# Byte stores of a top-k moved three steps later, and the first loads, masks and transpositions of the next stage one step sooner

## The chip, the cores and the metric

The kernel runs on one NeuronCore of a Trainium2 chip. The metric is the device time of one execution in microseconds (us). Engines are named as the profile names them: PE (matrix products and transpositions), DVE, ACT and POOL (elementwise work), SP (it issues nearly all DMA transfers here). PEclk is the TensorE clock that was granted, as a share of full speed.

## What is computed

One transformer layer over 2 x 1024 tokens of width 1024, inner width 2752. First a gated MLP whose gate keeps only the larger half of its values in each row, then a layernorm; then an MLP with low-rank additions, and a second layernorm.

```python
s = silu(einsum('bsh,ih->bsi', x, w_gate))
_, idx = top_k(-abs(s), k)                 # k = 2752 // 2, the smallest |s|
s = s.at[rows, idx].set(0.0)
s = s * einsum('bsh,ih->bsi', x, w_up)
h = layernorm(x + einsum('bsi,hi->bsh', s, w_down))
gate = silu(qlora(h, w1q, a1, b1))
y = qlora(gate * qlora(h, w3q, a3, b3), w2q, a2, b2)
out = layernorm(h + y)                     # qlora: tiled base weight plus 0.5 * h A^T B^T
```

All inputs are float32. The kernel splits each operand into a high and a low part and sums three products (high x high, high x low, low x high), so each product is issued three times.

## The kernel before

The 2048 tokens are 16 tiles of 128, in four groups of four (`GT = 4`). Three stages follow one another on PE.

**gate_up** walks a list of steps (group g, unit u, "g" or "u", k), with four units of 688 columns in a group. A unit has seven gate products (k = 0 to 6), formed with sums and differences of operands so that seven do the work of eight, and four up products (k = 0 to 3). L353 issues a product's matmuls of 344 columns: for each of two outputs eight with the high weight and the two parts of x alternately and, at the end, four with the low weight, as the code of `products` orders them; a step of an up product issues two such sets. Weights are loaded by SP into `wr` and split by ACT (`wh`, L173) and POOL (`wl`, L174). Four sums of weights (T1 to T4) were written to DRAM once and are read straight into `wh` and `wl` (L258). Results go to DRAM by SP (L387): `s_d`, the silu of the gate, and `m_d`, its product with the up part, not yet cut.

**The top-k** of a group is the generator `topk`. It finds for each row a threshold by passes that count (on ACT, DVE), one step of it being handed out per product step (L338 to L340; two at up products with even k), so that group g - 1 is thresholded while group g is multiplied. Its end: DVE writes one byte per value, keep or not (L513), into `kv`; then comes a section that all engines enter together, in which DVE reads a flag and a rare exact fallback may run (L530 to L534); then each of the group's four byte tiles is stored to DRAM, `k_d`, one store to a step (L536 to L539). The store is issued behind the last load that was noted (`lastd`). For the last group the same generator runs inside down: from item 12 of the first group on, one step to an item.

**down** multiplies by `w_down`. Its items are (block of inner width `DB`, tile), 24 to a group. An item loads a piece of `m_d` (L710) and of `k_d` (L711), turns the bytes to bf16 on ACT (L724), multiplies on POOL (L725), transposes on PE (L745), takes the high part `mh` on ACT (L749) and the low part `ml` on DVE (L750), runs the products against pieces of `w_down` (L765, 512 columns) and adds their sum to the accumulator on DVE (L768). The accumulator starts as a tile of x, loaded by SP (L775).

The first three items of down, the **early** ones, are prepared inside gate_up. `down(0, early=3)` is a generator that the last unit of the last group advances (L341 to L346). Its first `next` issues the loads of the three items; they go into slices of a tile `em` in the room of a buffer of the top-k (`a0`). The second issues their masks (L724, L725), the third their transpositions and the writing of `eh` and `el` (L745, L749, L750). Their products follow when down starts. Items 1 and 3 use the same PSUM tile for their transpositions.

After a group's last item comes a layernorm, and the finished tile is stored as `x_d`. When the last group's top-k has been used up, `dots_down` (L639, L815 to L838) begins: it reads `x_d` back and forms the row sums of the low-rank parts on DVE (L837), one or two steps to an item (L644, L645); what is left is run at L137, after the third group's items.

**ffn** is the second MLP; the change doesn't touch it.

The order of instructions on an engine isn't the order in the program: a scheduler with a model of time lays them out, within waits and a few `issue_after` conditions. Every engine and SP then works its own queue in order.

Of the kernel before, what the change touches and what calls it, by code (L numbers as in the profile page):

```python
# [26 lines left out]
NU = NB // 2  # L27
# [38 lines left out]
class Kern:  # L66
# [216 lines left out]
    def gate_up(self):  # L283
        nc, V = self.nc, self.nc.vector
        ng = self.nt // GT
        self.steps = [(g, u, w, k) for g in range(ng) for u in range(NU) for w in "gu" for k in range(7 if w == "g" and g + u else 4)]
        self.xfull, self.tkg, self.xs, self.xraw, self.wraw, self.wq, self.li, self.wi = {}, None, {}, {}, [], [], 0, 0
        cc, self.b0 = {}, {}
        pss = {}
        xg = self.x_raw(0)  # L290
        next(xg)
        for i, (g, u, w, k) in enumerate(self.steps):
            while self.li < min(i + LOADS + 1, len(self.steps)):
                self.w_load(self.li)
                if self.li == 0:
                    list(xg)
                self.li += 1
            while self.wi < min(i + AHEAD + 1, len(self.steps)):
                j = self.steps[self.wi]
                if j[:2] == (0, 0):  # L300
                    for op in {("g", 0): ("A11", "A21"), ("g", 1): ("A12", "A22")}.get(j[2:], ()):
                        self.x_slot(op)
                self.w_prep(self.wi)
                self.wi += 1
            wh, wl = (x.rearrange("p (a b) -> p a b", a=KH) for x in self.wq.pop(0))
            if self.form(i):
                a = GATE[k][0]
                ps = self.pair()[:, :, :BW]
                self.products([(ps[:, p], self.xs[p, a]) for p in range(NPR)], wh, wl, True, True)
                self.post((g, u), k, ps, cc)  # L310
            else:
                first = w == "g"
                h = int((G0 if first else UP)[k][1]) - 1
                n = int((G0 if first else UP)[k][2]) - 1
                st, sp = (k < 2, k > 1) if first else (h == 0, h == 1)
                if st:
                    ps = [self.pair()[:, :, :BW] for j in range(2)]
                    pss[n] = ps
                ps = pss[n]
                for j in range(2):  # L320
                    self.products([(ps[j][:, p], self.xs[p, f"A{j + 1}{h + 1}"]) for p in range(NPR)], wh, wl, st, sp)
                if sp:
                    (self.up if w == "u" else self.gate)((g, u), n, ps, cc)
            if g + u == 0 and w == "u" and k:
                with self.behind():
                    for op in (("S2",), ("S1", "S3"), ("S4",))[k - 1]:
                        self.x_slot(op)
            if u == NU - 1 and g + 1 < ng:
                if (w, k) == XAT["raw"][0]:
                    self.xg = self.x_raw(g + 1)  # L330
                for _ in range(XAT["raw"].count((w, k))):
                    next(self.xg, None)
                for op in XAT.get((w, k), ()):
                    with self.behind():
                        self.x_slot(op)
            if g and (u, w, k) == TKAT:
                self.tkg = self.topk(g - 1)
            for _ in range(2 if w == "u" and k % 2 == 0 else 1):  # L338
                if self.tkg:
                    next(self.tkg, None)  # L340
            if (g, u, w) == (ng - 1, NU - 1, "u") and k > 1:  # L341
                next(self.d0)
            if (g, u, w, k) == (ng - 1, NU - 1, "u", 1):
                self.et = [self.tk.tile([P, NI], d, tag=f"a{j}", name=n) for j, (n, d) in enumerate((("em", F), ("eh", R), ("el", R)))]
                self.d0 = self.down(0, early=3)
                next(self.d0)  # L346
# [70 lines left out]
    def topk(self, g, nact=3):  # L417
# [112 lines left out]
        with self.tc.tile_critical():  # L530
            r = V.value_load(fi[0:1, 0:1])
            with V.If(r != 0):
                for j in range(GT):
                    self.exact(av[j], kv[j], av[j - 1] if j else b, cand, x, c1, bit, half)  # L534
        self.lastd = self.lastv = self.lasta = self.lastp = None
        for j, t in enumerate(tiles):  # L536
            yield
            with self.tc.issue_after(self.lastd.ins) if self.lastd is not None else ExitStack():
                nc.sync.dma_start(self.k_d[t], kv[j])  # L539
# [552 lines left out]
```

## Time and profile before

| | us |
|---|---|
| three runs, median (lowest to highest) | 1924.16 (1921.65 to 1924.33) |
| the profiled execution | 1926.91 |
| its span | 1925.1 |
| mean granted clock of TensorE | 0.993 |
| L353, products of gate_up, PE busy | 610.4 + 609.8 + 342.1 |
| L765, products of down, PE busy | 217.8 + 215.1 + 205.5 |
| L174, low parts of weights, POOL busy | 566.4 |

The span runs from the first instruction to the last, and lies within the execution's time. Busy times of PE count pipelined matmuls, each of which overlaps the next: a matmul of 344 columns has a duration of 0.32, and one starts every 0.157. In a row of a timeline stand the start, the duration, engine, line, operation, output and inputs and how many, and in brackets the idle time before it and what ended it. In a row of waits stand the engine and line that waited, what it waited for, the total, the number of times and the longest. In a row of windows stand the stretch and its length, the busy time and number of instructions of PE, PE's weight loads, DVE, ACT and POOL, then the granted clock, the share of the DMA engines and GB/s.

### The profile page before, as it was taken

To read this page: it belongs to the slowest core of one execution; us is meant where nothing else is said; L and a number is where in the kernel's file an instruction comes from. 1 tells how busy PE (TensorE), PEld (TensorE's weight loads), DVE (VectorE), ACT (ScalarE), POOL (GpSimd) and SP (SyncE) were. 2 spreads that over 40 slices of the span, in tenths; PEclk is the share of its full clock that TensorE was granted. 3 is DMA by queue.
4 is the path that set the end of the run, shared out by engine and by line. 5 is a ranking of instruction groups with operands and counts; after the bars stand their busy time and mean duration, and the time that the engine had idled before them with its cause. 6 is when DMAs were issued, how large, how long until landed. Compare 5 with 4: busy or idle time off the path is not lost. (4 is left out here: it accounts for less than half of the span.)

```text
span 1925.1 us, 29381 instructions
## 1 busy us (share of the span) xinstructions
PE 1885.3 (98%) x10825; PEld 1754.4 (91%) x10825; DVE 1229.6 (64%) x1831; ACT 904.0 (47%) x1448; POOL 973.0 (51%) x606
## 2 busy tenths in 40 slices
PE   9999999999999999999999999999998999998998
PEld 9999999999999999999888787888787979898896
DVE  4633556767358574691238998688467857779565
ACT  4333477414883258622246533323333746557362
POOL 5655664445445354355565443554565746436062
PEclk9999999999999999999999999999999999999999
DMA  7677687676977868667798756977776878485651
GB/s 266 237 250 260 236 325 261 210 272 253 330 231 241 314 235 303 236 228 256 282 328 285 270 188 227 337 245 261 268 250 244 279 284 321 155 318 177 229 196 66
DMA packets 166205, 488.66 MB, mean 254 GB/s; under 512 B 24772, under 2 KB 45380, under 8 KB 166056
## 3 DMA queue, kind: packets, MB, share of 16 engines
q1 hardware_dynamic: 165848, 486.43, 71.9%
q8 instruction: 85, 1.39, 0.3%
q14 instruction: 64, 0.52, 0.1%
q10 hardware_dynamic: 208, 0.31, 0.0%
HBM read 370.30 MB, written 116.33 MB: 253 GB/s over the span
## 5 line engine op out<-in xcount | busy, mean ns | idle before, releaser
L174 POOL TENSOR_TENSOR wl<-wr,wh 128x1376 fp32r<-128x1376 f32 (+2 forms) x187 | 566.4, 3035 | 466.1 <-ACT wh L173 436.8
L353 PE MATMUL mm<-wh,xh 128*128 128x344 f32 x1928 | 610.4, 322 | 2.8 <-DMA wh<-tw3T1h 2.8
L353 PE MATMUL mm<-wh,xl 128*128 128x344 f32 x1928 | 609.8, 320 | 0.0
L173 ACT CAST wh<-wr 128x1376 fp32r<-128x1376 f32 (+2 forms) x192 | 232.4, 1215 | 340.9 <-PE mm L353 199.6
L353 PEld LDWEIGHTS mm<-wh,xh 128*128 128x128 f32 x1928 | 364.7, 189 | 3.0 <-issue 3.0
L353 PEld LDWEIGHTS mm<-wh,xl 128*128 128x128 f32 x1928 | 364.6, 189 | 0.0
L353 PE MATMUL mm<-wl,xh 128*128 128x344 f32 x1928 | 342.1, 319 | 0.0
L353 PEld LDWEIGHTS mm<-wl,xh 128*128 128x128 f32 x1928 | 310.1, 188 | 0.0
L765 PE MATMUL mm<-wh,mh 128*128 128x512 f32 x680 | 217.8, 400 | 0.1
L765 PE MATMUL mm<-wl,mh 128*128 128x512 f32 x680 | 215.1, 395 | 1.1 <-POOL wl L174 1.1
L765 PE MATMUL mm<-wh,ml 128*128 128x512 f32 x648 | 205.5, 396 | 0.8 <-DVE ml L750 0.8
L460 ACT ACTIVATE jk<-a,cur 128x2752 int8<-128x2752 f32 x66 | 170.8, 2588 | 31.2 <-DVE cur L482 15.8
L994 POOL TENSOR_TENSOR hf<-hf,gt 128x344 f32<-128x344 f32 x96 | 142.2, 1491 | 75.6 <-DVE gt L988 68.7
L725 POOL TENSOR_TENSOR m<-m,ub 128x512 f32<-128x512 f32 (+2 forms) x93 | 111.0, 1194 | 128.0 <-ACT ub L724 65.8
L981 PE MATMUL mm<-wh,fh 128*128 128x344 f32 x512 | 166.2, 325 | 5.8 <-DVE gt L988 5.2
L983 PE MATMUL mm<-wh,fl 128*128 128x344 f32 x512 | 164.0, 320 | 0.0
L982 PE MATMUL mm<-wl,fh 128*128 128x344 f32 x512 | 163.9, 320 | 0.0
L765 PEld LDWEIGHTS mm<-wl,mh 128*128 128x128 f32 x680 | 127.4, 188 | 30.1 <-POOL wl L174 2.2
L768 DVE TENSOR_TENSOR acc<-acc,mm 128x1024 f32<-128x1024 f32 x96 | 116.4, 1214 | 57.9 <-PE mm L765 27.8
L765 PEld LDWEIGHTS mm<-wh,mh 128*128 128x128 f32 x680 | 124.7, 189 | 24.8 <-ACT mh L749 0.5
L765 PEld LDWEIGHTS mm<-wh,ml 128*128 128x128 f32 x648 | 121.2, 189 | 26.9 <-DVE ml L750 1.0
L992 ACT ACTIVATE pa<-pa 128x344 f32<-128x344 f32 x256 | 123.0, 483 | 38.6 <-DVE pa L990 34.0
(191 smaller groups left out, 2742.5 us busy)
## 6 DMA issues: line engine op xcount, KB each, us to landing
wr<-wu SPq DMA_DIRECT2D x64, 688.0 KB
wr<-wg SPq DMA_DIRECT2D x52, 688.0 KB
wr<-wd SPq DMA_DIRECT2D x48, 512.0 KB
s_d<-cc SPq DMA_DIRECT2D x64, 344.0 KB
m_d<-mt SPq DMA_DIRECT2D x64, 344.0 KB
a<-s_d SPq DMA_DIRECT2D x64, 344.0 KB
wl<-wc_w SPq DMA_DIRECT2D x48, 344.0 KB
wh<-wc_w SPq DMA_DIRECT2D x48, 344.0 KB
```

Of the source, the lines that this page charges most:

```text
L173: self.lasta = self.nc.scalar.copy(hi, raw)
L174: (eng or self.nc.gpsimd).tensor_tensor(lo, raw, hi.bitcast(F), ALU.subtract)
L353: self.nc.tensor.matmul(o, l, r, start=start and n < m and n % (2 * KH) == 0, stop=stop and n >= m and (n - m) % KH == KH - 1)
L460: nc.scalar.activation(jk.bitcast(I8), av[j], AF.Sign, bias=t, scale=-1.0, accum_out=s)
L725: nc.gpsimd.tensor_tensor(m[:, :w], m[:, :w], ub[:, :w], ALU.mult)
L765: nc.tensor.matmul(ps[:, h], a, b[:, h * 512 : (h + 1) * 512], start=i == 0, stop=i == len(ops) - 1)
L768: nc.vector.tensor_tensor(out, out, ps.rearrange("p a b -> p (a b)"), ALU.add)
L981: nc.tensor.matmul(o, fh[:, c, :], wh[:, c, :], start=c == 0, stop=False)
L982: nc.tensor.matmul(o, fh[:, c, :], wl[:, c, :], start=False, stop=False)
L983: nc.tensor.matmul(o, fl[:, c, :], wh[:, c, :], start=False, stop=False)
L992: nc.scalar.activation(pa[:, r], pa[:, r], AF.Copy, scale=0.5, accum_out=part[:, r, b : b + 1])
L994: G.tensor_tensor(hf[:, hs], hf[:, hs], gt, ALU.add)
```

## The change

Two edits. In `gate_up` the generator of the early down items is created and first advanced at up product k = 0 of the last unit instead of k = 1, and advanced again at k = 1 and 2 instead of 2 and 3. In `topk` three empty steps stand ahead of the four stores of bytes, so that each store is handed out three steps later, in gate_up as well as in down.

```diff
@@ gate_up
-            if (g, u, w) == (ng - 1, NU - 1, "u") and k > 1:
+            if (g, u, w) == (ng - 1, NU - 1, "u") and k in (1, 2):
                 next(self.d0)
-            if (g, u, w, k) == (ng - 1, NU - 1, "u", 1):
+            if (g, u, w, k) == (ng - 1, NU - 1, "u", 0):
                 self.et = [self.tk.tile([P, NI], d, tag=f"a{j}", name=n) for j, (n, d) in enumerate((("em", F), ("eh", R), ("el", R)))]
                 self.d0 = self.down(0, early=3)
                 next(self.d0)
@@ topk
         self.lastd = self.lastv = self.lasta = self.lastp = None
+        yield
+        yield
+        yield
         for j, t in enumerate(tiles):
             yield
             with self.tc.issue_after(self.lastd.ins) if self.lastd is not None else ExitStack():
                 nc.sync.dma_start(self.k_d[t], kv[j])
```

## The prediction

> **What bounds the kernel now.** I read the page's busy times first, then PE's waits, then the two places where these waits lie, as windows and as timelines.
>
> ```profile
> PE 1885.3 (98%) x10825; PEld 1754.4 (91%) x10825; DVE 1229.6 (64%) x1831; ACT 904.0 (47%) x1448; POOL 973.0 (51%) x606
> ...
> PE mm L353 <- DMA wh<-tw3T1h: 2.8, 1, 2.8
> PE mm L765 <- POOL wl L174: 2.5, 4, 1.4
> PE mm L745 <- DVE el L750: 1.9, 1, 1.9
> ...
> SPq L539 <- DVEq L530: 34.5, 4, 9.9
> ```
>
> PE is busy for 98% of the span. Some 35 to 40 us (1925.1 - 1885.3) are all that a change of order can win, plus what a lowered clock costs. Three of PE's waits are at work that this diff moves: the weight tile T1h (2.8), the early transposes (1.9) and the first down product (1.4). SP stands before the byte stores four times, 9.9 us at the longest; for the third top-k it stands until 870.93.
>
> ```profile
> 870.93 2.14 SPq L539 DMA_DIRECT2D k_d<-ku  x4
> 873.12 0.81 SPq L710 DMA_DIRECT2D em<-m_d  x1
> 873.99 0.85 SPq L711 DMA_DIRECT2D em<-k_d  x1
> 874.93 0.90 SPq L387 DMA_DIRECT2D m_d<-mt  x2
> 875.87 0.58 SPq L710 DMA_DIRECT2D em<-m_d  x1
> 876.55 0.66 SPq L258 DMA_DIRECT2D wh<-tw3T1h  x1
> ...
> 882.62 0.63 PE L353 MATMUL mm<-wh,xh 128*128 128x344 f32 x1 [2.79 <-DMA wh<-tw3T1h]
> ...
> 879.00:882.50 3.50, 0.83 (x6) 0.55 (x4) 0.88 (x1) 0.00 (x0) 0.41 (x1) 1.00 1.01 338
> 882.50:886.00 3.50, 3.38 (x12) 3.41 (x13) 0.00 (x0) 0.00 (x0) 0.00 (x0) 0.52 0.97 334
> ```
>
> **Place A.** After 870.93 SP issues a backlog, and nine transfers stand ahead of T1h. The DMA share is 1.01, so they are served at full load. PE runs dry for 2.79 us, and the last row shows the second cost: the granted clock is 0.52 for the next 3.5 us.
>
> ```profile
> 929.54 1.03 PE L745 MATMUL mm<-ident,em 128*128 128x128 f32 x8
> 932.47 0.63 PE L745 MATMUL mm<-ident,em 128*128 128x128 f32 x4 [1.90 <-DVE el L750]
> 934.54 1.19 PE L765 MATMUL mm<-wh,eh 128*128 128x512 f32 x2 [1.45 <-POOL wl L174]
> 935.54 1.05 PE L765 MATMUL mm<-wl,eh 128*128 128x512 f32 x2
> ...
> 941.06 0.63 PE L765 MATMUL mm<-wh,el 128*128 128x512 f32 x2
> ```
>
> **Place B**, the handoff from gate_up to down. The twelve early transpositions stand at the very end of gate_up. The third item's four share a PSUM tile with the first item's, so they wait for its `el` (L750), and the first product waits for the third item's `el`: the page names wl, but that was written some 25 us earlier, while the last `el` ends at 933.75 + 0.69 = 934.44, 0.1 before the product. Then the clock is low: pairs of products start 0.85 to 1.0 apart until 940.59, afterwards 0.46.
>
> **The change, part by part.**
>
> *Early preps one step sooner (L341).* In the order of the build, eight transpositions now stand between the k=2 and k=3 up products, the other four some 30 matmuls into k=3 (30 x 0.157 = 4.7 us later), and L765 follows the last L353 directly. The transpositions' own time (1.03 + 0.63) stays. Both waits go: 1.90 + 1.45 = **3.35 us**; `el` of items 1 and 2 took 1.29 on DVE, inside the 4.7. The low clock goes too: seven pairs took 940.59 - 934.54 = 6.05 instead of 7 x 0.465 = 3.25, so **2.8 us**. Late next would be wl of the later weight tiles: the fourth is needed after nine pairs, 4.2 us behind the first product, and comes about 2.7 us after gate_up's end (SP's wd load that waits for it starts at 932.23, gate_up ends at 929.5), which fits. Sum -6.15. Ends: 0 if another operand holds the first product for as long, -6.15 otherwise; I take the latter, since the other operands' rows end 10 to 25 us early.
>
> The masks move with them (ACT L724, 3 x 0.61; POOL L725, 3 x 1.16); both engines keep their order there, and m was ready 25 us before its transposition. Nothing for these.
>
> Here a rule speaks against the change. The Trainium skill, "TensorE: Matmul & The Clock Gate", Part 4, says that transpositions don't count as PE-busy the same way. They would then put 1 us of seeming idleness into the product stream. With its Part 1 (half clock after an idle window of about 3.4 us, and about 3.4 busy us to recover), 1.03 us is too little to lower the clock: 0 by the rule as well. The row: four transpositions amid products around 946.8 and 948.4 leave the clock at 0.99 in 940 to 960. I take 0. Part 1 matters more at A: 2.79 us is less than its window, so by the rule alone the removal may be worth 2.79 only. The trace has clock 0.52 after that gap, while the 2.7 us wait for POOL m (L725) at 1194 left 1.00. Where the row is, it decides: the sixteen matmuls from 882.62 took 4.08 (to 886.70) instead of 16 x 0.158 = 2.53, so 1.55 more.
>
> *Stores three steps later (L535) and the six em loads one step sooner (L343): T1h.* Store 0 is still first behind SP's wait, so SP still starts at 870.93. Then all six em loads stand before T1h, but three stores stand behind it. It has nine transfers ahead as before. Their bytes, with the sizes of section 6: before 4 x 344 KB (k_d) + 2 x 256 + 64 (em) + 2 x 344 (m_d) = 2.64 thousand KB; after 344 + 3 x 256 + 3 x 64 + 688 = 1.99. That is 0.65 thousand KB = 0.67 MB less, at 338 GB/s 2.0 us. SP's issues (0.44 to 0.9 each) put T1h at 876.6 as before, so it can't land before about 880. The wait becomes 0.8 (2.79 - 2.0), and a gap so short should not lower the clock: **-2.0 - 1.55 = -3.5**. Ends: 0, if the smaller em packets cost what the stores did; -4.35, if both costs vanish. T4h now has one store ahead of it and PE comes 3.5 us sooner, but it was issued 13 us before its use. No new wait.
>
> In groups 1 and 2 the same stores move behind the loads of the next weights. PE has 20.00 of 20 us at 400 to 440 and at 640 to 680, before as well: nothing to win there, and SP order loosens. 0.
>
> *What the sooner PE meets.* At 947.04 DVE's L768 waits 12.60 for acc<-x, issued by SP at 940.72 behind wd loads. It frees the PSUM tile that item 3 needs. Before, PE came to item 3 at 955.31. Now it comes about 9.7 us sooner, while the SP chain shifts only with A (3.5), so L768 ends near 948.26 - 3.5 = 944.8 and PE comes near 945.6; with one or two us of slip in SP's queue, and DMA at 1.03 of its share in 940 to 960, I count **+2**. Ends 0 and +5.2 (all of B except the waits' last us).
>
> *Top-k of the last group, in down.* There the three extra yields are items: the stores leave three items later, and `dots_down` (L639) starts three items later. About 24 instead of 29 of its 36 steps are handed out before the drain at L137, so five more dots of 1.22 us fall into the last items: 6.1 us of DVE where DVE already has 19.86 of 20 us (1300 to 1320). PE's cover there is about 4 to 5 us, so **+1**; ends 0 and +6. The stores of this group are read only in down(3): 0.
>
> *Everything behind down(0)* is laid out anew by the scheduler. DVE is at 17 to 20 of 20 us in 1020 to 1180, PE has 20.00 nearly throughout; ml's margins there are 1 us and less. I count 0, ends -3 and +4.
>
> Sum: -6.15 - 3.5 + 2 + 1 = -6.65. On the profiled execution (1926.91; its span 1925.1 plus 1.8 around it) this gives 1920.3; that execution is 2.75 above the median of the runs, 1924.16. So **1917.5**.
>
> **The rivals.**
> 1. *The handoff gain is handed back.* PE waits at item 3 and on the m loads behind it for what SP and a full DMA bring at the old time: +5.2 instead of +2, so 1920.7, at the edge of no change. For it: 12.60 of waiting for acc<-x. Against: m and weight operands behind have 4 to 5 us of margin, and buffers are released by PE itself.
> 2. *A stays.* Six small-row loads ahead of T1h take as long as the stores did: 1917.5 + 3.5 = 1921.0. For it: DMA moves only 250 to 270 GB/s around 878, where em loads run. Against: the em bytes before T1h grow by 0.4 MB while the stores shrink by 1.1. That the change does not do what it says is the same case: SP's 9.9 us before store 0 remain.
> 3. *Slower.* In 1040 to 1180 DVE works through the top-k in passes of 3.0 to 3.5 us (L463, L497, L513, L500). Where the new order puts one more pass ahead of an item's `ml` (L750), that item's transposed operand is 3 us later against a margin of about 1: 2 us of PE each. Fewer than three such items leave it faster; from about six on, 12 us, it gives 1929. For it: DVE's share. Against: the passes are handed one per item, and the order of the build shows at most one pass between neighbouring ml and acc operations there, as before.
>
> **How the numbers follow.** Forecast 0.50, rival 1 0.17, rival 2 0.15, rival 3 0.13; both first rivals together 0.05 (1924.2). A measurement of this kernel tells about 0.2%, 3.85 us, from no change: below 1920.3 is faster, above 1928.0 slower. Faster: 0.47 of the forecast and half or less of rivals 1 and 2: 0.61. Slower: rival 3 and a little of the order behind down(0): 0.14. Same: 0.25. The range goes from 1912.5 (no give-back, A's whole 4.35, some us from the new order) to 1926 (both first rivals with a few us of dots). The forecast alone spans 1913 to 1921.
>
> **What would show it.** L353's wait for T1h under 1 us and clock 1.00 after it; no wait of L745 for el and none of the first L765; pairs 0.46 apart from the first. A new wait of L765 or L745 near item 3 is the give-back. PE under 20.00 in 1040 to 1180 or 1290 to 1330 would show the DVE costs. I am wrong if T1h's wait stays near 2.8, or if new waits behind 1000 add more than 6 us.

## The result, and the profile after

The changed kernel takes 1939.37 us (median of 5 runs, 1937.36 to 1942.07), the kernel before 1921.65 in the same rounds: a ratio of 1.0092, 95% interval 1.0079 to 1.0106. It is 17.7 us slower; 1917.5 had been forecast.

The profiled execution took 1937.36, its span is 1935.6. The lines behind L535 are three higher than before. The busy times on the page of the changed kernel:

```profile
PE 1884.5 (97%) x10825; PEld 1753.8 (91%) x10825; DVE 1224.2 (63%) x1831; ACT 903.7 (47%) x1448; POOL 974.1 (50%) x606
```

Its waits of PE and, in the last row, of SP (engine and line, what it waited for, total, times, longest):

```profile
PE mm L768 <- ACT mh L752: 6.3, 7, 2.1
PE tp L748 <- POOL m L728: 5.0, 1, 5.0
...
PE mm L353 <- DMA wh<-tw3T1h: 4.3, 1, 4.3
PE mm L768 <- DVE z L586: 3.3, 1, 3.3
...
SPq L542 <- DVEq L530: 28.1, 4, 9.7
```

PE does the same work (1884.5 us), so the time is idle time, with some lowered clock behind it. The wait for T1h is there, and longer. The waits of L745 for `el` and of the first product are gone. Three waits are new: those for ACT's `mh`, one of 5.0 for POOL's mask and one of 3.3 for DVE. SP's longest stand before the byte stores is what it was (9.7 against 9.9).

The two early places of the changed kernel, as a timeline of SP and PE (start, duration, engine, line, operation, tiles, count, and in brackets the idle time before it):

```profile
871.15 0.32 SPq L542 DMA_DIRECT2D k_d<-ku  x1
871.52 0.66 SPq L713 DMA_DIRECT2D em<-m_d  x1
...
875.70 1.40 SPq L258 DMA_DIRECT2D wh<-tw3T1h  x1
...
884.22 0.63 PE L353 MATMUL mm<-wh,xh 128*128 128x344 f32 x1 [4.25 <-DMA wh<-tw3T1h]
...
924.51 1.03 PE L748 MATMUL mm<-ident,em 128*128 128x128 f32 x8
930.12 0.60 PE L748 MATMUL mm<-ident,em 128*128 128x128 f32 x4
933.39 0.63 PE L768 MATMUL mm<-wh,eh 128*128 128x512 f32 x2
933.86 0.62 PE L768 MATMUL mm<-wl,eh 128*128 128x512 f32 x2
```

At the first place the order is the predicted one, one store and six `em` loads before T1h. T1h's issue began 0.85 earlier than before and ended at about the same time (877.10 against 877.21); it landed 1.6 later. What had changed is the rate of the DMA engines while the `em` loads ran (the last number of a row, GB/s). The kernel before, and then the changed one:

```profile
874.00:875.00 1.00, 1.00 (x9) 1.00 (x8) 0.00 (x0) 0.17 (x1) 1.00 (x1) 1.00 1.04 388
875.00:876.00 1.00, 1.00 (x8) 1.00 (x7) 0.00 (x0) 1.00 (x1) 0.67 (x1) 1.00 0.93 247
```

```profile
874.00:875.00 1.00, 1.00 (x8) 1.00 (x8) 0.00 (x0) 0.04 (x1) 1.00 (x1) 1.00 0.94 257
875.00:876.00 1.00, 1.00 (x8) 1.00 (x7) 0.00 (x0) 1.00 (x1) 0.80 (x1) 1.00 0.86 124
```

Over 872 to 877 the rate was 358 GB/s before and 251 after. At the second place the transpositions stand inside the products, nothing waits, and the pairs start 0.47 apart from the first: as predicted.

To see where the time went, the table compares when PE started the same matmul in two traces. Against a second execution of the kernel before (`before_again`, span 1918.7), a second one of the changed kernel (`after_again`, span 1935.7) is

| place, by the time before | later by, us |
|---|---|
| end of the T1h place, 893 | -1.3 |
| behind the handoff, 945 | -6.4 |
| behind the fourth item, 965 | -2.7 |
| 1046 | +1.1 |
| 1330 | +2.2 |
| 1340 | +7.3 |
| 1410 | +5.9 |
| 1441 | +18.6 |
| end | +17.0 |

So all that PE has won by the handoff (-6.4, of which 1.3 at T1h) is handed back by 1046; the loss is made in two stretches far behind the edits, 5.1 us at 1330 to 1340 and 12.7 at 1410 to 1441.

### The profile page after: what moved, and what is told of

Read it like the earlier page. It is cut to its first block, busy times and chain, and to the rows that moved or that the text cites. A ratio compares the mean times of both kernels' runs of the same rounds, so it can differ in the third digit from the quotient of the medians.

```text
span 1935.6 us, 29377 instructions
## 1 busy us (share of the span) xinstructions
PE 1884.5 (97%) x10825; PEld 1753.8 (91%) x10825; DVE 1224.2 (63%) x1831; ACT 903.7 (47%) x1448; POOL 974.1 (50%) x606
```

## Experiments

Each ratio is to the kernel before, in runs of the same chip. Each diff says which kernel it starts from.

### The parts of the change alone

`e1_stores_only` keeps only the three empty steps (L535). From the changed kernel:

```diff
-            if (g, u, w) == (ng - 1, NU - 1, "u") and k in (1, 2):
+            if (g, u, w) == (ng - 1, NU - 1, "u") and k > 1:
-            if (g, u, w, k) == (ng - 1, NU - 1, "u", 0):
+            if (g, u, w, k) == (ng - 1, NU - 1, "u", 1):
```

> The three empty steps ahead of the byte stores are kept, the early loads, masks and transpositions are back at their old steps. Theory 1 (the stores' steps cost, at two places: T1h behind six em loads in gate_up, about +2.4, and the tail, where ACT stands for an own transfer near 1425, about +7 to +10): 9 to 14 us slower than before, PE waits over 3.5 us for T1h, handoff waits of 1.9 and 1.45 at the first transpositions and product return, and ACT stands for br<-braw some 10 us near 1430. Theory 2 (the early preparation costs, because PE runs ahead of what down's other queues bring): within 3 us of before. Theory 3 (any new order costs, wherever it comes from): about 10 us slower, but with waits at other places.

`e2_early_only` has the opposite: the change's L341 and L343, without the empty steps.

> Only the early loads, masks and transpositions are one step sooner; no empty steps ahead of the stores. Theory 1: faster than before by 1 to 5 us: the wait for T1h stays at 2.8, the two handoff waits and the low clock behind them go (-6.15), a new wait of about 1.8 at the fourth item, and up to 4 us are handed back in waits for ACT's mh (L749) near 1024 to 1045; the tail behind 1350 as before. Theory 2: 8 to 15 us slower. Theory 3: 5 to 10 us slower.

`e3_no_down_yields` is the whole change, with the empty steps in the top-k of the first three groups alone (it is called with `nact` 3 there and 2 in down). From the changed kernel:

```diff
-        yield
-        yield
-        yield
+        for _ in range(3 if nact == 3 else 0):
+            yield
```

> As the changed kernel, but the three empty steps are left out in the last group's top-k, which runs inside down. Theory 1: the T1h wait of 4.3 stays and the early gain too, the tail returns to the order of before: within 3 us of before, 13 to 18 faster than the changed kernel, no wait of ACT over 7 us near 1430. Theory 2: as the changed kernel, 13 or more slower than before. Theory 3: 5 to 10 us slower.

`e4_down_yields_only` is the kernel before with the empty steps in the last group's top-k alone (`0 if nact == 3 else 3`).

> Only the three empty steps in the last group's top-k, inside down; the top-k of the other groups and the early items as before. Theory 1: most of the loss is here: 7 to 13 us slower, with the dots' wait of about 3 near 1335 and ACT standing near 1430; all before 1190 as before. Theory 2: within 3 us of before. Theory 3: 5 to 10 us slower.

| kernel | median | ratio (95%) |
|---|---|---|
| e1, empty steps everywhere | 1936.40 | 1.0073 (1.0049 to 1.0098) |
| e2, early items | 1924.66 | 1.0010 (0.9997 to 1.0023) |
| e3, early items, empty steps in gate_up | 1925.51 | 1.0016 (1.0005 to 1.0027) |
| e4, empty steps in down | 1937.63 | 1.0081 (1.0055 to 1.0108) |

The loss is in the empty steps inside down: about 14.7 of 17.7 us (e4 against 1922.90). The early items alone change nothing that can be told from zero, where I had expected 1 to 5 us of gain. In gate_up the later stores cost nothing measurable. Two more expectations missed: e1's wait for T1h was 2.2 and not over 3.5, and e4 lost more than the 7 to 13 us.

### By what the steps in down cost

Three things stand behind them: the later byte stores themselves, the row sums of `dots_down`, which start three items later, and what follows these. `e9_before_dots_late` is the kernel before with the row sums alone delayed. From the kernel before:

```diff
 def dots_down(self):
+        for _ in range(5):
+            yield
         for i in range(4):
             yield
```

> The kernel before, with five empty steps ahead of the row sums of dots_down, so that twelve of their steps instead of seven are left when the third group's items end; byte stores and early items untouched. Theory 1a (the loss comes from the row sums that are left over, which move the order of everything behind them): 12 to 16 us slower than before, with a wait of PE for DVE of 3 to 5 near 1335 and ACT standing some 10 us for br<-braw near 1430, as in the changed kernel. Theory 1b (the later stores themselves cost, through SP's queue or what waits for them): within 3 us of before.

It takes 1935.30, 1.0061 (1.0046 to 1.0076): 12.3 us slower, though stores and early items are those of before. `e5_dots_two_an_item` goes the other way, with the whole change. From the changed kernel:

```diff
-                for _ in range(2 if n % 2 else 1):
+                for _ in range(2):
                     next(self.dg, None)
```

> The changed kernel whole, but the row sums of dots_down are handed out two to every item instead of two and one in turn, so that the three items of delay are made up and only about four steps are left over. Theory 1a: the loss goes but for the two early places, which cancel: within 4 us of before, 11 to 17 faster than the changed kernel; ACT doesn't stand over 7 us near 1430. Theory 1b: still 12 or more slower than before.

It takes 1924.94, 1.0011 (1.0001 to 1.0021): the loss is gone, with the byte stores as late as in the change. The rows of windows show both stretches (busy time and count of PE, PE's loads, DVE, ACT and POOL; granted clock; DMA share; GB/s). First the second execution of the kernel before:

```profile
1320.00:1340.00 20.00, 20.00 (x97) 16.42 (x97) 14.31 (x39) 10.20 (x14) 9.55 (x12) 1.00 0.87 308
1420.00:1440.00 20.00, 20.00 (x96) 16.51 (x95) 12.70 (x23) 6.93 (x12) 11.94 (x16) 1.00 0.83 306
```

Then the second execution of the change:

```profile
1320.00:1340.00 20.00, 16.74 (x77) 13.34 (x76) 20.00 (x43) 3.80 (x5) 7.18 (x10) 0.99 0.48 177
1420.00:1440.00 20.00, 15.38 (x65) 12.15 (x64) 12.51 (x14) 3.65 (x8) 10.90 (x8) 0.91 0.96 281
```

Then e9, where only the row sums are late:

```profile
1320.00:1340.00 20.00, 17.47 (x75) 13.95 (x74) 19.56 (x50) 5.49 (x8) 8.76 (x11) 0.92 0.62 224
1420.00:1440.00 20.00, 15.98 (x65) 12.44 (x64) 12.01 (x15) 4.66 (x10) 10.81 (x10) 0.91 1.00 317
```

And e5, the change with denser row sums:

```profile
1320.00:1340.00 20.00, 20.00 (x92) 16.37 (x92) 17.69 (x44) 7.09 (x9) 9.19 (x12) 1.00 0.68 239
1420.00:1440.00 20.00, 20.00 (x98) 16.48 (x98) 12.64 (x25) 6.35 (x12) 11.93 (x15) 1.00 0.94 320
```

With twelve row sums left over DVE is full at 1320 to 1340 (14.31 of 20 us before) and PE loses three us; and in both kernels PE misses about a third of its matmuls at 1420 to 1440, at a lowered clock. With denser row sums both stretches are whole. So the cause is what is left of the row sums when the third group ends: making the same remainder without the change makes the loss, and removing it from the change removes the loss.

`d4_eleven_left` and `d2_nine_left` are e9 with four and two empty steps; `r1_before_dots_two` is the kernel before with two row-sum steps an item, so that none are left. Theory 3b goes by the order of transfers in the build; no trace shows which earlier transfer an issue waits for.

> The kernel before with four empty steps ahead of the row sums: eleven are left at the end of the third group. In the order of this build the last of ACT's transfers br<-braw do not share a place in the ring of transfers with a load of w_down, but with a load of x2a. Theory 3a (the size of the leftover decides: about 2.5 us of loss for each step beyond seven): 8 to 11 us slower than before. Theory 3b (what decides is whether ACT's transfer has to wait for a load of w_down issued just before it): within 4 us of before, ACT waits under 5 us near 1430.

> The same with two empty steps: nine are left. Here the last of ACT's transfers does wait for a load of w_down (and the one ahead of it for a load of x2a). Theory 3a: 4 to 6 us slower than before. Theory 3b: 6 to 12 us slower, with ACT standing 7 us or more near 1430.

> The kernel before, with the row sums handed out two to every item, so that none are left over; nothing else. If the leftover costs in the kernel before as well: 1 to 4 us faster than before. If its seven steps are hidden, as PE's 20.00 us at 1300 to 1340 say: within 2 us.

| steps left over | kernel | median | ratio (95%) |
|---|---|---|---|
| 0 | r1 | 1919.63 | 0.9982 (0.9974 to 0.9990) |
| 7 | before | 1922.68 | 1 |
| 9 | d2 | 1926.07 | 1.0019 (1.0011 to 1.0028) |
| 11 | d4 | 1932.76 | 1.0049 (1.0031 to 1.0066) |
| 12 | e9 | 1935.30 | 1.0061 (1.0046 to 1.0076) |

The loss grows with the leftover, by 1.7 to 2.5 us for each step beyond seven, where such a step takes 1.22 us on DVE. By the size alone (3a) d4 was expected at 8 to 11 us and took 10.1, d2 at 4 to 6 and took 3.4, a little under. By theory 3b d4 should have lost under 4 and d2 6 to 12: it fails in both. **r1 is 3.1 us faster than the kernel before**, so handing out the row sums more densely helps there too, though by less than half a us for each of the seven steps. That these steps themselves were the cost isn't shown: r1's trace ends 2.0 ahead of `before_again`, and 1.5 of that is already there at 893, behind the wait for T1h, where r1's clock stayed up.

### The second stretch

In the changed kernel's trace the second stretch starts on ACT. SP, ACT, POOL and PE in turn:

```profile
1421.85 1.59 SPq L606 DMA_DIRECT2D wr<-wd  x3
...
1423.48 0.47 ACT L752 CAST mh<-tp 128x384 fp32r<-128x384 f32 x1
1431.04 2.74 ACTq L816 DMA_DIRECT2D br<-braw  x2
1433.88 0.51 ACT L727 CAST ub<-u 128x384 bf16<-128x384 uint8 x1 [9.93 <-DMA br<-braw]
...
1422.52 1.92 POOL L174 TENSOR_TENSOR braw<-braw,br 128x344 fp32r<-128x344 f32 x1
...
1434.47 0.91 POOL L728 TENSOR_TENSOR m<-m,ub 128x384 f32<-128x384 f32 x1 [9.15 <-ACT ub L727]
...
1435.44 0.68 PE L748 MATMUL tp<-ident,m 128*128 128x128 f32 x3 [5.00 <-POOL m L728]
1435.77 1.22 PE L768 MATMUL mm<-wh,mh 128*128 128x512 f32 x2
1436.79 1.05 PE L768 MATMUL mm<-wl,mh 128*128 128x512 f32 x2
```

ACT issues the small transfers of the FFN's constants itself, and here it stands 7 us before it issues two of them, though POOL had their data ready at 1422.52 + 1.92 = 1424.44. The stand lies just behind a burst of weight loads on SP, with the DMA share at 1.00 (1420 to 1430); what ended it no row names. The mask's conversion is queued behind them, so POOL is late, so PE waits 5.0 and then runs pairs 0.85 to 1.0 apart. `e6_br_by_sp` is the change with these transfers on SP. From the changed kernel:

```diff
-                nc.scalar.dma_start(self.br[w + 2 : w + 4, bs].bitcast(F), lo[w + 2 : w + 4, :].bitcast(F))
+                nc.sync.dma_start(self.br[w + 2 : w + 4, bs].bitcast(F), lo[w + 2 : w + 4, :].bitcast(F))
```

> The changed kernel, but the sixteen small transfers br<-braw (L816) are issued by SP instead of ACT. Theory 2a (PE's loss near 1430 is ACT standing for its own transfer, behind which the masks' conversions wait): 6 to 12 us faster than the changed kernel, no wait of 5 for POOL's m near 1435. Theory 2b (ACT's standing is a symptom; the masks come late because their loads and the weights' loads fill the DMA engines there): within 3 us of the changed kernel.

It takes 1930.65, 1.0039 (1.0024 to 1.0054): 7.7 of the 17.7 us are left. But d4 loses 8 to 9 us at 1410 to 1420 in another way: ACT stands before a transfer of its own there too, but only until 1414.46, and then waits on for the bytes of the mask (`u<-k_d`) until 1416.90; PE waits 3.7 for the `mh` behind them. So ACT's transfer is how the changed kernel loses most of it, not the only way.

The constants take the room of the row sums, and the first `br<-braw` starts at 1366.9 before and 1374.6 after. Whether this lateness is the path was tried from both sides. `s1_after_consts_two` hands out the steps of `ffn_consts` twice (L641) in the changed kernel; `s2_before_consts_late` puts two empty steps ahead of them in the kernel before; `s3_dots_consts_two` is r1 with the constants two to an item:

> The changed kernel, with the steps of ffn_consts handed out two to an item, so that the constants, which wait for the row sums' room, catch up with the items; the twelve row sums left over stay. Theory 4a (the leftover costs because it makes the constants and ACT's sixteen transfers late): 8 to 15 us faster than the changed kernel, within 6 of before, with the wait of PE near 1338 still there. Theory 4b (the leftover costs in another way, through what the row sums and the layernorm behind them make late on DVE): within 4 us of the changed kernel.

> The kernel before, with two empty steps ahead of the constants: they start two items, some 10 us, later, as in the changed kernel, but with seven row sums left over as before. Theory 4a: 8 to 14 us slower than before. Theory 4b: within 3 us of before.

> The kernel before, with row sums and constants both handed out two to an item. If the constants' place still costs where no row sum is left over (theory 4a): 1 to 5 us faster than with the row sums alone, that is 4 to 8 faster than before. If not: within 2 us of that one, 3 faster than before; if the denser constants crowd ACT and SP, slower than that.

s1 took 1936.99, 1.0072 (1.0055 to 1.0090), no better than e1 or e4; s2 1921.12, 0.9989 (0.9981 to 0.9997), if anything faster; s3 1927.15, 1.0017 (1.0007 to 1.0027), slower than r1. The theory of late constants falls, by s1 above all: its last `br<-braw` start at 1419.5, where the changed kernel's start at 1431.0, and the loss is still there. s2 tests less than it was meant to: its first `br<-braw` comes at 1371.1, 4 us later than before and not 10, and its last at 1418.7, no later than before (1421.9). In s1 5.0 us are lost at 1330 to 1340, as in the change, but the rest of its loss lies at 1350 to 1380 and 1410 to 1440 in waits of 1.6 to 2.6. The second loss comes with the leftover and moves with the order; which engine hands it on in every case stays open.

### Two tries at a better kernel, and two second executions

`r2_early_dots_two` is r1 with the early items of the change; `v1_dots_two_consts_late` is r1 with s2's two empty steps.

> The early items one step sooner and the row sums two to every item, without the empty steps ahead of the stores. If the early items' gain is handed back near 955 and 1024 to 1045 as in the run with them alone: within 3 us of before. If it was handed back only because of what stood behind: 3 to 6 us faster.

> The kernel before, with row sums two to an item and two empty steps ahead of the constants: the two edits that were each a little faster alone. If their gains (3 and 2 to 3 us) lie at different places: 4 to 6 us faster than before. If both come from the same room on DVE and ACT behind 1300: about 3 faster, as with the row sums alone.

r2: 1922.50, 1.0001 (0.9987 to 1.0014), 2.9 slower than r1: the early items don't help there either. v1: 1921.81, 0.9992 (0.9982 to 1.0002), 1.4 faster than before, less than either expectation: the two gains don't add.

`after_again` and `before_again` are the two kernels unaltered, for second traces.

> The changed kernel unaltered, for a second trace. If the wait for T1h is set by the order of SP's queue, it is 4.3 again within 0.4; if it depends on the execution, it lies anywhere between 2 and 4.5, as in the four variants (2.2 and 4.1 with this order, 3.2 twice with the order of before). The tail near 1430 loses 10 again.

> The kernel before unaltered, for a second trace. If the waits of 2.8 for T1h and 2.7 for POOL's m near 1194 are set by the order, both come again; if they depend on the execution, at least one differs by over 1. The first trace's execution lay 4 us above the median of all runs.

They took 1937.45 and 1920.51. The changed kernel's wait for T1h, in the second execution:

```profile
PE mm L353 <- DMA wh<-tw3T1h: 2.0, 1, 2.0
```

It was 4.3 in the first, with one and the same order of SP's queue. Over all traces the order of before gives 2.7 to 3.5 (twelve traces, mean 3.1), the order of the change 1.8 to 4.3 (seven traces, mean 2.8). In before's second trace the wait of 2.7 near 1194 is missing, the one for T1h is 2.8 again.

## Why the prediction was wrong

**The failed step** is the one on the top-k of the last group in down, +1 with ends 0 and +6, together with the next, "I count 0, ends -3 and +4" for all that is laid out anew. The mechanism of the first was right: five more row sums on a full DVE. Its size was not. The cover of 4 to 5 us that I gave PE at 1300 to 1320 belonged to another place. Before, the last row sum stands ahead of the third group's layernorms, which start at 1320.52:

```profile
1317.64 1.22 DVE L837 SCALAR_TENSOR_TENSOR dj<-dx,db 128x1024 uint8<-128x1024 f32 x1
```

In the changed kernel the last four stand among these layernorms, and at 1330 to 1340 one product waited for the `ml` behind them (the row names L586, but the product starts 0.05 after this `ml` ends at 1338.41):

```profile
1330.49 1.22 DVE L840 SCALAR_TENSOR_TENSOR dj<-dx,db 128x1024 uint8<-128x1024 f32 x1
1337.73 0.68 DVE L753 TENSOR_TENSOR ml<-tp,mh 128x512 fp32r<-128x512 f32 x1
...
1334.71 0.48 PE L768 MATMUL mm<-wl,mh 128*128 128x512 f32 x1
1338.46 0.73 PE L768 MATMUL mm<-wh,ml 128*128 128x512 f32 x2 [3.27 <-DVE z L586]
```

By the table above, of the second executions, the same matmul is 5.1 later behind this place than ahead of it: a wait of 3.3 and a lowered clock behind it. And the term had no second part: another 11 (12.7 until 1441, of which 1.6 come back by the end). Together it measured 12 to 15 us (e9, e4) instead of 1. I had asked what the leftover costs where it runs, and not what it does to the order and the waits of the next 100 us.

**Place A**, -3.5, measured nothing that can be told from zero: e3 differs from e2 by 0.85 us of the median. The order came as predicted and T1h was issued no later than predicted, but the wait is 2.8 in the mean instead of 0.8. The term divided the 0.67 MB saved by 338 GB/s, a rate from behind these loads (879 to 882.5). Where the six `em` loads run the rate was lower than before, 251 instead of 358 over 872 to 877; in these five us that is 0.5 MB less moved, so the lower rate takes back most of what fewer bytes won. Of four traces with this order, whose queues start at about the same time, the two with 251 and 258 (e3) waited 4.3 and 4.1, and the two with 276 (the second execution) and 283 (e1) waited 2.0 and 2.2; why the rate differs between executions of one order is open. Nor was the clock spared: behind the waits of 2.0 and 1.8 (the latter in e6) it was 0.58 and 0.52 at 883 to 886. This was the second rival.

**Place B**, -6.15: right. In `e2_early_only` both waits and the low clock are gone, and the same matmul, 1.5 later than in the first trace of before ahead of the handoff (910), is 5.0 earlier behind it (945): 6.5. **The give-back**, +2: right at the fourth item (a wait of 2.1 for the accumulator's sum in e2), but a second one came, 3 us at 1024 to 1045, where ACT's `mh` is late in the new order. In the trace some 5.5 are given back by 1046, about the first rival's +5.2, but more than half of it at a place that the rival did not name. By the medians the early items gain nothing.

**The slow rival** had the right sign and the right engine, DVE, at the wrong place: at 1040 to 1180, where it was put, the changed kernel loses little (+1.1 at 1046, +2.2 at 1330). That the stores in groups 1 and 2 cost nothing was right.

The parts add up: early items +1.8 (e2), stores in gate_up +0.9 (e3 less e2) and steps in down +14.7 (e4) make 17.4; the change measured 17.7.

## What to carry to other kernels

Where steps of a background job are handed out by the step of a main loop, count what is left at the end of the loop before and after an edit that delays it: the remainder runs in one burst, and its price is not its own duration. An edit to the order of one stage is to be priced in the stage that takes over, too; a variant that makes the same remainder in another way, as e9 does, shows this with one line. And a gain at a handoff is only worth what the stage behind it can take up.

## What the runs showed of the hardware

The clock did not follow the length of the idle time. The same stretch of windows (the granted clock is the third number from the end) in e6, whose wait for T1h was 1.8, and in r1, where it was 2.9:

```profile
883.00:886.00 3.00, 3.00 (x13) 3.00 (x12) 0.00 (x0) 0.08 (x1) 0.00 (x0) 0.52 1.03 420
```

```profile
883.00:886.00 3.00, 2.95 (x19) 2.66 (x18) 0.00 (x0) 0.50 (x1) 0.00 (x0) 1.00 0.97 341
```

Of nineteen traces eighteen have a lowered clock behind this wait, whether of 1.8 or 4.3, and r1 has none. Nor did one program always do the same: the changed kernel's wait near 1338 was 3.27 in the first execution and 3.26 in the second, and over 1340 to 1343 the clock was 1.00 in the one and 0.52 in the other. In these traces the length of a wait between 1.8 and 4.3 us does not tell whether the clock falls behind it.

A transfer of 688 KB with nine others ahead of it landed 2.3 us apart, counted from its issue, in two executions of one program. And ACT, which issues small transfers of its own, stood 6 to 8 us before it issued two of them (changed kernel and e9), with its other work queued behind.
